# A two-layer graph kernel: the first layer in two parts, two list copies moved behind the first keys, later keys further ahead

## The chip, the cores and the metric

The kernel runs on one core of one Trainium2 chip. The metric is the device time of one execution in microseconds (us), lower is better. The kernel before has a median of 1617.65 us over three runs (1616.7 to 1618.55).

## The reference, cut to what matters

There are N = 6250 nodes with 64 features each, and E = 200000 edges given as two lists of integers, `src` and `dst`; `dst` is sorted. The first block is a two-layer SAGE network with a residual and a layer norm:

```
def sage_conv(x, src, dst, W_l, b_l, W_r, n_nodes):
    msg = x[src]
    agg = segment_sum(msg, dst, num_segments=n_nodes)
    cnt = segment_sum(ones, dst, num_segments=n_nodes)
    return agg / maximum(cnt, 1.0) @ W_l.T + b_l + x @ W_r.T
h   = relu(sage_conv(x, src, dst, W_l1, b_l1, W_r1, n))
x   = layernorm(x + sage_conv(h, src, dst, W_l2, b_l2, W_r2, n))
```

The second block has three message layers. Each sums `concat(x[dst], x[src], edge_attr) @ W.T + b` over the edges of every destination, with a batch norm between layers, a residual and a last layer norm. Every layer therefore sums over the same edges: five times the same sparse matrix, the count A[src, dst] of edges, is applied to node features.

## The kernel before, in words

**The matrix.** The kernel builds A once, as small 8-bit floats, in 13 tiles of 512 destinations each (`adj8`, in DRAM), and applies each tile to all nodes with matmuls (`aggregate`, line 664). Node features are held as three bf16 parts (`parts`), so that the sums stay exact enough.

**The build.** Edges are taken in slots of 128. One matmul per slot (line 1008) multiplies a one-hot of the low 7 bits of the source (`lo`) by a one-hot of a combined key of destination and high bits of the source (`rhs`), and adds into a PSUM pair of banks, `pair`; ScalarE copies a finished pair into the tile `a` (lines 1015 and 1020). VectorE makes the one-hots (`one_hots`, line 626) with a comparison of an iota with the keys, one instruction for 16 slots (`lo`) or for a run of slots (`rhs`). There are three buffers each of `lo` and `rhs`, and two of `pair`.

**The keys.** Slots go in 21 groups t of 128. For each group `fetch(t)` reads the edges (two gathers on GpSimd, DMA_INDIRECT of line 892), and `columns(t)` turns them into keys: four instructions on VectorE (lines 901 to 904), two TensorE transposes into `lin` (line 909) and one ScalarE copy into `k2` (line 911), which the one-hots read. Where each slot starts in the sorted list is searched at run time, in five steps of the list `SEARCH`: `near_samples` (line 826, then `pos` in line 834), `gather_behind` (GpSimd gathers, line 839), and `first_edges` (a comparison and sum per group, line 848, then `start_i` in line 860). `fetch(0)` reads the inputs `dst` and `src` themselves; later ones read padded copies of them in DRAM, `ends`, which two DMAs make at the start (line 798), one from the SP queue and one from the ACT queue. The features x come after the first keys (`load_x`, line 808, SP queue).

`on_slot` decides at which slot of which group these steps are called:

```
if c == (32 if t == 0 else 0):        # first_edges, fetch(t + 1), near_samples, gather_behind, gather_dst
...
if c == (96 if t == 0 else 64) and t + 1 < R:
    columns(t + 1)
```

**The first layer beside the build.** When step u of the build is written, the first SAGE layer of the tile finished before it follows in the source: `first_layer` aggregates (196 matmuls into `agg`), VectorE copies the counts (line 725), adds the three parts (line 689), divides (726, 727, 733); then four transposes (714), `lin` (736), a ScalarE relu (738), four matmuls (742) and a split into bf16 parts by ScalarE and TensorE in turn (636, 638). x itself is split the same way in `split_x` (line 882) between slots 64 and 192.

**Who sets the order.** The source order is not the order on the engines. A scheduler merges the program with a cost model of its own and may move an instruction past others of its engine; instructions wrapped in `pin` keep their order among themselves. Each engine then runs its instructions strictly in that fixed order and waits on semaphores. So the changed lines act through the order that results. The order of both programs on each engine is known before they run.

**After the build** (from about 485 us) come the last two first layers, the second SAGE layer with the edge attributes (to about 916 us), and the three message layers, which are almost nothing but matmuls.

Of the kernel before, what the change touches and what calls it, by code (L numbers as in the profile page):

```python
# [11 lines left out]
F32 = mybir.dt.float32  # L12
# [10 lines left out]
P = 128  # L23
# [451 lines left out]
def gnn_kernel(ctx: ExitStack, tc: tile.TileContext, x, src, dst, ea, W_l1, b_l1, W_r1, W_l2, b_l2, W_r2,  # L475
# [10 lines left out]
    nc = tc.nc  # L486
    pin = tc.keep_in_program_order
    N, D = x.shape
    E, EC = ea.shape
# [9 lines left out]
    def tw(j):  # L499
        return min(TW, NPAD - j * TW)  # L500
# [9 lines left out]
    R = -(-NS // P)  # L510
    subs = []
    for b in range(NB):
        n, c = slots_for(expected(N, E, b * P, (b + 1) * P)), 0
# [27 lines left out]

    dram = ctx.enter_context(tc.tile_pool(name="fdram", bufs=1, space=DRAM))
    ends = [dram.tile([E + PADE, 1], I32, name=f"ends{i}") for i in range(2)]
    adj8 = [dram.tile([P, NB * tw(j)], mybir.dt.uint8, name=f"adj8_{j}") for j in range(NT)]
    ok_t = None

    with ExitStack() as fast:
# [12 lines left out]
        parts = [const.tile([P, NB, 3 * D + 2], BF16, name="parts0"), const.tile([P, NB, 3 * D], BF16, name="parts1")]  # L560
# [157 lines left out]


        def first_layer(psa1, a, j):  # L720
            w, s = tw(j), slice(j * TW, j * TW + tw(j))
            nb, bs = w // P, j * TW // P
            ps, = aggregate(psa1, parts[0], [(a, j)], 3 * D + 1)
            c, ic = cnt[:, bs: bs + nb], inv[:, bs: bs + nb]
            nc.vector.tensor_copy(c, ps[:, :nb, 3 * D])
            nc.vector.tensor_single_scalar(ic, c, 1.0, ALU.max)
            nc.vector.reciprocal(ic, ic)
            nd = work.tile([P, 4, P], F32, name="nd")
            own_x = nc.scalar.copy(nd[:, :nb, D:], res[:, bs: bs + nb, :])
            if j == order[0][0]:  # L730
                pin(own_x)
            add_parts(nd[:, :nb, :D], ps, nb)
            nc.vector.tensor_mul(nd[:, :nb, :D], nd[:, :nb, :D], ic.unsqueeze(2).to_broadcast([P, nb, D]))
            mx = transposed_tile(nd, nb)
            ph = psm.tile([P, TW], F32, name="lin")
            nc.tensor.matmul(ph[:, :w], w1s, mx[:, :w], start=True, stop=True)
            h1 = work.tile([H1, TW], F32, name="h1")
            nc.scalar.activation(h1[:, :w], ph[:, :w], AF.Relu, bias=bl1)
            pz = psm.tile([P, 4, P], F32, name="tr")
            for i in range(nb):  # L740

                nc.tensor.matmul(pz[:, i, :], h1[:, i * P: (i + 1) * P], w2s, start=(i == 0), stop=True, skip_group_check=True)
            split_psum(parts[1][:, bs: bs + nb, :], pz[:, :nb, :D])
            nc.vector.tensor_add(res[:, bs: bs + nb, :], pz[:, :nb, D:], res[:, bs: bs + nb, :])


        with ExitStack() as bld:
# [15 lines left out]
            psa1 = slots.enter_context(tc.tile_pool(name="fpsa1", bufs=1, space=PSUM))  # L763
# [29 lines left out]
                pin(nc.scalar.dma_start(end[E:, :].rearrange("(p c) o -> p (c o)", p=64), pad[:64, i, :]))  # L793
            low = parts[1].rearrange("p b c -> p (b c)").bitcast(F32)
            early_weights = load_weights(low)
            for end, of, eng in ((ends[0], dst, nc.sync), (ends[1], src, nc.scalar)):

                pin(eng.dma_start(end[0: E, :].rearrange("(c p k) o -> p c (k o)", p=16, k=500),
                                  of.rearrange("(c p k) -> p c k", p=16, k=500)))
            nc.gpsimd.memset(parts[0][:, :, 3 * D: 3 * D + 1], 1.0)  # L800
            smf = pp.tile([EP, NSMP], F32, name="smf")
            nc.vector.tensor_copy(smf, smp)
# [1 line left out]
            def load_x():  # L804

                pin(nc.vector.memset(res[:, NB - 1, :], 0.0))
                pin(nc.vector.memset(res[:, :, 0:1], 0.0))
                pin(nc.sync.dma_start(res[:, : NB - 1, :], x[0: (NB - 1) * P, :].rearrange("(b p) d -> p b d", p=P)))
                pin(nc.sync.dma_start(res[:LASTB, NB - 1, :], x[(NB - 1) * P:, :]))
# [75 lines left out]
            cols, fetched, late_weights = {}, {}, []  # L885
# [10 lines left out]
            def columns(t):  # L896

                rows = fetched.pop(t)
                hi = ew.tile([P, P], I32, name="hi", bufs=1)
                key = ew.tile([P, 2, P], F32, name="key")  # L900
                pin(nc.vector.tensor_single_scalar(hi, rows[:, 1, :], 7, ALU.logical_shift_right))
                nc.vector.scalar_tensor_tensor(key[:, 0, :], rows[:, 0, :], float(NB), hi, ALU.mult, ALU.add)
                nc.vector.scalar_tensor_tensor(key[:, 1, :], hi, -float(P), rows[:, 1, :], ALU.mult, ALU.add)
                nc.vector.tensor_scalar(key[:, 0, :], key[:, 0, :], tab[:, 2, t: t + 1], 2000.0, ALU.subtract, ALU.min)  # L904
                if t == 0:
                    nc.vector.tensor_add(key[:, 0, :], key[:, 0, :], passed)
                kp = psm.tile([P, 2, P], F32, name="lin")
                for i in range(2):
                    nc.tensor.transpose(kp[:, i, :], key[:, i, :], ident)
                k2 = ew.tile([P, 2, P, 2], F16, name="k2")  # L910
                nc.scalar.copy(k2, kp.unsqueeze(3).to_broadcast([P, 2, P, 2]))  # L911
                cols[t] = k2, {}
                cols.pop(t - 2, None)

            def on_slot(slot):

                t, c = divmod(slot, P)
                if c == (32 if t == 0 else 0):
                    for g, (*_, t1) in enumerate(SEARCH):
                        if t == t1:  # L920
                            first_edges(g)
                            if g == len(SEARCH) - 1:
                                first_attributes()
                    if t + 1 < R:
                        fetch(t + 1)
                    for g, (_, _, t0, _) in enumerate(SEARCH):
                        if t == t0:
                            near_samples(g)
                            gather_behind(g)
                    gather_dst(t)  # L930
                if c == (96 if t == 0 else 64) and t + 1 < R:
                    columns(t + 1)
                    if t == 0:
                        for to, of in early_weights:
                            transposed(to, of)

                if t == SEARCH[-1][3] + 1 and c == 0:
                    free[0] = parts[1].rearrange("p b c -> p (b c)").bitcast(F32)
                    late_weights.extend(load_message_weights(spare))
                if t == SEARCH[-1][3] + 2 and c == 0:  # L940
                    for to, of in late_weights:
                        transposed(to, of)
                k = slot // HOT - 4
                if 0 <= k < 8 and c % HOT == 0:
                    n = -(-NB // 4)
                    split_x(k * n // 8, (k + 1) * n // 8)
# [5 lines left out]
            fetch(0)  # L952
            gather_behind(1)
            columns(0)
            load_x()
            pin(nc.sync.dma_start(thr[:, early:], t_ap[:, early:].to_broadcast([EP, P * (R + 1) - early])))
            pin(nc.sync.dma_start(etab, e_dram.ap() if hasattr(e_dram, "ap") else e_dram))

            def lo_hot(t, c):
                k2, made = cols[t]  # L960
                if c // HOT not in made:
                    lo = hot.tile([P, HOT, P], BF16, name="lo")
                    one_hots(lo, k2[:, 1, c // HOT * HOT: (c // HOT + 1) * HOT, :], iota)
                    made[c // HOT] = lo
                return made[c // HOT][:, c % HOT, :]

            built = {}

            def build(u):

# [5 lines left out]
                a = built[j]  # L976
# [21 lines left out]
                for e, (slot, wc, bank, col, first, last) in enumerate(todo):  # L998
                    t, c = divmod(slot, P)
                    wp = wc + wc % 2  # L1000
                    e0, g, i = of_run[e]
                    on_slot(slot)
                    if i == 0:
                        rhs = hot.tile([P, RUN], BF16, name="rhs")[:, : g * wp].rearrange("p (g n) -> p g n", n=wp)
                        one_hots(rhs, cols[t][0][:, 0, c: c + g, :], iota)
# [75 lines left out]
            for u, (j, _, _) in enumerate(order):  # L1081
                a = build(u)
                if u == 10:
                    relative_dst()
                if u == len(order) - 1:
                    break
                if prev is not None:
                    first_layer(psa1, *prev)
                    ready.append(prev[1])
                prev = (a, j) if a is not None else None  # L1090
            slots.close()
            psa = fast.enter_context(tc.tile_pool(name="fpsa", bufs=2, space=PSUM))
            psb = bld.enter_context(tc.tile_pool(name="psb", bufs=2, space=PSUM))
            for a, j in (prev, (a, j)):
                first_layer(psa, a, j)
                ready.append(j)


# [182 lines left out]
```

## Time and profile before

| | us |
|---|---|
| median of three runs | 1617.65 |
| the profiled execution, its own time | 1620.58 |
| span in that profile (first to last instruction) | 1618.8 |
| TensorE busy in the span | 1498.8 |
| VectorE busy | 886.1 |
| ScalarE busy | 574.3 |
| GpSimd busy | 226.9 |

The profiled execution lies 2.93 us, or 0.18%, above the median. "Busy" adds up the time in which an engine had an instruction running; a wait is written to the instruction that waited and to what ended the wait. The time of GpSimd's DMA_INDIRECT rows is the time in which it writes descriptors, not that of the transfer.

### The profile page before, as it was taken

To read this page: it belongs to the slowest core of one execution; us is meant where nothing else is said; L and a number is where in the kernel's file an instruction comes from. 1 tells how busy PE (TensorE), PEld (TensorE's weight loads), DVE (VectorE), ACT (ScalarE), POOL (GpSimd) and SP (SyncE) were. 2 spreads that over 40 slices of the span, in tenths; PEclk is the share of its full clock that TensorE was granted. 3 is DMA by queue.
4 is the path that set the end of the run, shared out by engine and by line. 5 is a ranking of instruction groups with operands and counts; after the bars stand their busy time and mean duration, and the time that the engine had idled before them with its cause. 6 is when DMAs were issued, how large, how long until landed. Compare 5 with 4: busy or idle time off the path is not lost.

```text
span 1618.8 us, 38661 instructions
## 1 busy us (share of the span) xinstructions
PE 1498.8 (93%) x17213; PEld 1384.0 (85%) x17213; DVE 886.1 (55%) x1462; ACT 574.3 (35%) x1080; POOL 226.9 (14%) x95
## 2 busy tenths in 40 slices
PE   3888799999998989999999999999999999999997
PEld 2676688888886888999899988889899999899997
DVE  6899998988969409987986511111431111442222
ACT  3737476777848404544554100000310000310000
POOL 2565732731610100000000000000000000000000
PEclk9897899999999999999999999999999999899998
DMA  5312232320321635435344354443245444264540
GB/s 134 122 30 95 46 100 88 158 93 14 157 84 81 240 133 223 182 130 206 133 145 154 126 239 160 167 171 120 124 187 212 162 163 156 101 240 175 193 163 10
DMA packets 45200, 227.32 MB, mean 140 GB/s; under 512 B 23621, under 2 KB 31650, under 8 KB 37343
## 3 DMA queue, kind: packets, MB, share of 16 engines
q1 hardware_dynamic: 37965, 139.40, 22.9%
q10 hardware_dynamic: 4306, 78.10, 12.3%
q0 software_dynamic: 2752, 7.26, 1.5%
q8 instruction: 136, 2.23, 0.5%
q14 instruction: 41, 0.34, 0.1%
HBM read 183.77 MB, written 42.57 MB: 140 GB/s over the span
## 4 chain that ended last, share of the span: by engine, by line
PE 64%; DVE 17%; issue 8%; ACT 6%; DMA 3%; POOL 2%; DVEq 0%; ACTq 0%; POOLq 0%
PE agg L664 48%; DVE lo L626 7%; PE pair L1008 7%; ACT a L1015 3%; DVE rhs L626 2%; PE u L1161 2%; DVE e L1066 2%; PE bank L1075 1%; POOL parts L839 1%; DMA e<-in_edge_attr_dram 1%; PE agg L671 1%; DVE e L1068 1%; DMA a<-adj 1%; DVE nd L689 1%; PE lin L1182 1%
## 5 line engine op out<-in xcount | busy, mean ns | idle before, releaser
L664 PE MATMUL agg<-parts,a 128*128 128x192 bf16 (+1 forms) x12005 | 1091.9, 246 | 6.3 <-DMA a<-adj 4.2
L664 PEld LDWEIGHTS <-a 128*128 128x128 fp8e3 x12005 | 1007.9, 98 | 25.7 <-issue 12.1
L1015 ACT ACTIVATE a<-pair 128x784 fp8e3<-128x784 f32 (+3 forms) x355 | 294.4, 900 | 107.2 <-PE pair L1008 85.8
L1008 PE MATMUL pair<-rhs,lo 128*128 128x147 bf16 (+5 forms) x2569 | 263.3, 239 | 45.0 <-ACT a L1015 15.3
L1008 PEld LDWEIGHTS <-lo 128*128 128x128 bf16 x2569 | 194.4, 101 | 98.8 <-issue 50.3
L626 DVE TENSOR_TENSOR rhs<-iota,k 128x1960 bf16<-128x1960 f16 (+15 forms) x240 | 239.2, 1018 | 18.3 <-ACT k L911 10.5
L626 DVE TENSOR_TENSOR lo<-iota,k 128x2048 bf16<-128x2048 f16 x161 | 195.3, 1217 | 1.9 <-ACT k L911 1.3
L689 DVE TENSOR_REDUCE z<-agg 128x256 f32<-128x768 f32 (+1 forms) x39 | 35.3, 910 | 282.6 <-PE agg L664 282.3
L892 POOL DMA_INDIRECT rows<-ends,start_i x40 | 142.6, 3564 | 177.6 <-DVE key L904 150.1
L626 DVE TENSOR_TENSOR lo<-iota,e_d 128x2048 bf16<-128x2048 f16 (+11 forms) x132 | 130.9, 1011 | 19.7 <-PE bank L1075 17.6
L1075 PE MATMUL bank<-lo,lhs 128*128 128x128 bf16 x1701 | 107.5, 219 | 18.0 <-ACT lhs L1069 12.6
L1075 PEld LDWEIGHTS <-lhs 128*128 128x128 bf16 x1701 | 98.3, 98 | 29.6 <-ACT lhs L1069 20.8
L689 DVE TENSOR_REDUCE nd<-agg 128x256 f32<-128x768 f32 (+1 forms) x26 | 23.5, 906 | 116.0 <-PE agg L664 116.0
L1177 POOL TENSOR_TENSOR nd<-res,inv 128x256 f32<-128x256 f32 (+1 forms) x13 | 7.6, 588 | 557.5 <-DVE inv L1152 346.6
L1169 DVE BATCH_NORM_STATS2 stats<-hr 64x6 f32<-64x512 f32 (+1 forms) x26 | 17.0, 653 | 101.7 <-ACT hr L1184 80.4
L716 ACT COPY mx<-tr 128x512 f32<-128x512 f32 (+1 forms) x26 | 14.7, 565 | 162.5 <-PE tr L714 162.5
L705 ACT ACTIVATE sp_r<-z 128x256 f32<-128x256 f32 (+1 forms) x26 | 10.5, 403 | 172.2 <-DVE z L704 172.0
L1198 ACT ACTIVATE hr<-tr 64x512 f32<-64x512 f32 (+1 forms) x13 | 7.3, 565 | 179.9 <-PE tr L1197 179.9
L839 POOL DMA_INDIRECT parts<-in_dst_dram,pos x22 | 60.8, 2763 | 40.8 <-DVE pos L834 31.7
L1065 ACT CAST lhs<-e 128x512 bf16<-128x512 f32 (+21 forms) x72 | 36.1, 503 | 64.0 <-PE bank L1075 40.5
L1066 DVE TENSOR_TENSOR e<-e,lhs 128x512 f32<-128x512 f32 (+21 forms) x72 | 39.4, 551 | 15.2 <-ACT lhs L1065 14.9
L1069 ACT CAST lhs<-e 128x512 bf16<-128x512 f32 (+21 forms) x72 | 36.4, 505 | 23.0 <-DVE e L1068 22.5
(145 smaller groups left out, 817.7 us busy)
## 6 DMA issues: line engine op xcount, KB each, us to landing
a<-adj SPq DMA_DIRECT2D x24, 3136.0 KB, 15.3
a<-adj ACTq DMA_DIRECT2D x24, 3136.0 KB, 11.1
adj<-a SPq DMA_DIRECT2D x12, 3136.0 KB, 9.6
e<-in_edge_attr_dram SPq DMA_DIRECT2D x25, 256.0 KB, 5.0
a<-adj SPq DMA_DIRECT2D x4, 784.0 KB, 4.1
out_dram<-z SPq DMA_DIRECT2D x12, 128.0 KB, 6.0
e<-in_edge_attr_dram SPq DMA_DIRECT2D x7, 152.0 KB, 3.6
adj<-a SPq DMA_DIRECT2D x1, 784.0 KB
```

What stands on the lines that cost most here:

```text
L626: nc.vector.tensor_tensor(to.rearrange("p g (h two) -> p g h two", two=2), iota[:, :n].rearrange("p (h two) -> p h two", two=2).unsqueeze( ...
L664: nc.tensor.matmul(sums[k][:, i, :n], views[k][:, b, i * P: (i + 1) * P], pt[:, b, :n], start=(b == sources[0] and terms is None and not ( ...
L689: nc.vector.tensor_reduce(to, ps[:, :nb, : 3 * D].rearrange("p b (r d) -> p b d r", r=3), AX.X, ALU.add)
L839: pin(nc.gpsimd.indirect_dma_start(out=blks[t % most], out_offset=None, in_=dst.rearrange("(e o) -> e o", o=1), in_offset=bass.IndirectOff ...
L892: pin(nc.gpsimd.indirect_dma_start(out=rows[:, i, :], out_offset=None, in_=end, in_offset=bass.IndirectOffsetOnAxis(ap=start_i[:, t: t + 1 ...
L1008: nc.tensor.matmul(pair[:, bank % 2, col: col + wc], lo_hot(t, c), rhs[:, i, :wc], start=first, stop=last)
L1015: nc.scalar.activation(av[:, :, o: o + 2 * nd].rearrange("p h (two d) -> p h two d", two=2), pair[:, :, : nd * NB].rearrange("p two (d h) ...
L1065: nc.scalar.copy(lhs[:, :g, 0:EC], r)
L1066: nc.vector.tensor_sub(r, r, lhs[:, :g, 0:EC])
L1069: nc.scalar.copy(lhs[:, :g, 2 * EC:3 * EC], r)
L1075: nc.tensor.matmul(ps[:, :P], lhs[:, q, :], oh[:, q % HOT, :], start=(c == 0 and q == 0), stop=(i == last_b[b] and q == g - 1))
L1161: nc.tensor.matmul(u[:, i, :], y[:, i * P: (i + 1) * P], maps[n - 1], start=True, stop=True)
```

## The change

It has four parts.

1. `first_layer` now returns after the aggregation, and the rest of it (counts, mean, transposes, both linear maps, the split) is a function that is called a quarter of the way into the next step of the build. The copy of the counts is pinned.
2. The two copies of `dst` and `src` into `ends` are no longer issued at the start. They are issued after `columns(0)`, both on the SP queue, behind a small DMA that writes one column of the first keys to DRAM (`seen`) and so makes the SP queue wait for those keys. `load_x` follows them on the same queue.
3. In group 0, the step with `first_edges`, `fetch(1)` and `near_samples` is called at slot 16 and not at slot 32.
4. From group 9 on, the keys of the next group are made at slot 32 and not at slot 64.

```diff
+    seen = dram.tile([P, 1], F32, name="seen")
...
         def first_layer(psa1, a, j):
+            ps, = aggregate(psa1, parts[0], [(a, j)], 3 * D + 1)
+            return lambda: first_layer_rest(ps, j)
+
+        def first_layer_rest(ps, j):
             w, s = tw(j), slice(j * TW, j * TW + tw(j))
             nb, bs = w // P, j * TW // P
-            ps, = aggregate(psa1, parts[0], [(a, j)], 3 * D + 1)
             c, ic = cnt[:, bs: bs + nb], inv[:, bs: bs + nb]
-            nc.vector.tensor_copy(c, ps[:, :nb, 3 * D])
+            pin(nc.vector.tensor_copy(c, ps[:, :nb, 3 * D]))
...
-            for end, of, eng in ((ends[0], dst, nc.sync), (ends[1], src, nc.scalar)):
-
-                pin(eng.dma_start(end[0: E, :].rearrange("(c p k) o -> p c (k o)", p=16, k=500),
-                                  of.rearrange("(c p k) -> p c k", p=16, k=500)))
+            def copy_ends():
+
+                pin(nc.sync.dma_start(seen, cols[0][2]))
+                for end, of in zip(ends, (dst, src)):
+                    pin(nc.sync.dma_start(end[0: E, :].rearrange("(c p k) o -> p c (k o)", p=16, k=500),
+                                          of.rearrange("(c p k) -> p c k", p=16, k=500)))
...
-                cols[t] = k2, {}
+                cols[t] = k2, {}, key[:, 0, 0:1]
...
-                if c == (32 if t == 0 else 0):
+                if c == (16 if t == 0 else 0):
...
-                if c == (96 if t == 0 else 64) and t + 1 < R:
+                if c == (96 if t == 0 else 64 if t < 9 else 32) and t + 1 < R:
...
             columns(0)
+            copy_ends()
             load_x()
...
                     on_slot(slot)
+                    if e == len(todo) // 4 and rest:
+                        rest.pop()()
...
                 if prev is not None:
-                    first_layer(psa1, *prev)
+                    rest.append(first_layer(psa1, *prev))
                     ready.append(prev[1])
                 prev = (a, j) if a is not None else None
+            for r in rest:
+                r()
...
             for a, j in (prev, (a, j)):
-                first_layer(psa, a, j)
+                first_layer(psa, a, j)()
                 ready.append(j)
```

More of the change, by code (lines that the diff above doesn't have):

```diff
@@ L959, in lo_hot @@
             def lo_hot(t, c):
-                k2, made = cols[t]
+                k2, made, _ = cols[t]
                 if c // HOT not in made:
@@ L967, in gnn_kernel @@
             built = {}
+            rest = []
             def build(u):
```

## The prediction, made before the changed kernel ran

> **What bounds the kernel now.** I read the windows first, because the change touches only the first 485 us and a mean over the kernel would hide it. Columns: stretch, its length, busy time (and count) of TensorE, weight load, VectorE, ScalarE, GpSimd, then the granted TensorE clock, DMA share and GB/s.
>
> ```profile
> 0.00:22.00 22.00, 2.40 (x22) 1.44 (x22) 6.15 (x35) 1.87 (x2) 8.67 (x19) 1.00 0.43 126
> 22.00:80.00 58.00, 45.10 (x414) 33.34 (x414) 50.27 (x79) 39.84 (x78) 24.80 (x15) 0.88 0.43 131
> 80.00:190.00 110.00, 88.61 (x1099) 74.77 (x1100) 108.04 (x172) 53.54 (x69) 69.83 (x22) 0.88 0.18 59
> 190.00:485.00 295.00, 283.16 (x3115) 252.15 (x3114) 260.52 (x318) 210.71 (x315) 107.44 (x25) 0.99 0.26 97
> ```
>
> To 22 us nothing is busy: a chain of small steps and DMAs leads to the first keys. From 22 to 190 us VectorE is the limit (158.3 of 168 us); TensorE idles 34 us there. From 190 us TensorE is (283 of 295). So a microsecond won at the start or on VectorE before 190 us should reach the end; one won on VectorE later should not. The waits of TensorE from 190 to 485 us confirm it: it waits for VectorE 1.6 us in all, in four rows.
>
> ```profile
> PE agg L664 <- DVE nd L689: 0.8, 2, 0.6
> PE pair L1008 <- DVE lo L626: 0.6, 2, 0.4
> PE tr L638 <- ACT parts L636: 0.2, 1, 0.2
> PE pair L1008 <- DVE rhs L626: 0.2, 1, 0.2
> ```
>
> Then the timeline of VectorE and GpSimd where VectorE does wait before 80 us (start, length, engine, what; in brackets the wait):
>
> ```profile
> 6.44 1.26 POOL L839 DMA_INDIRECT parts<-in_dst_dram,pos  x1 [3.66 <-DVE ext L826]
> 13.58 0.63 DVE L848 TENSOR_SCALAR_CACHE_REDUCE parts<-parts,tab 128x400 bf16<-128x400 int32 x1 [5.25 <-DMA parts<-in_dst_dram,pos]
> 16.54 0.94 POOL L892 DMA_INDIRECT rows<-in_src_dram,start_i  x1 [0.30 <-issue]
> 19.01 0.29 DVE L901 TENSOR_SCALAR hi<-rows 128x128 int32<-128x128 int32 x1 [3.59 <-DMA rows<-in_src_dram,start_i]
> ...
> 39.24 3.81 POOL L892 DMA_INDIRECT rows<-ends,start_i  x1 [16.76 <-DVE start_i L860]
> 45.83 0.28 DVE L901 TENSOR_SCALAR hi<-rows 128x128 int32<-128x128 int32 x1 [3.60 <-DMA rows<-ends,start_i]
> ...
> 66.65 6.58 POOL L839 DMA_INDIRECT parts<-in_dst_dram,pos  x1 [0.30 <-issue]
> 79.60 0.63 DVE L848 TENSOR_SCALAR_CACHE_REDUCE parts<-parts,tab 128x400 bf16<-128x400 int32 x1 [2.20 <-issue]
> ```
>
> Three waits count: 5.25 us for the first gather, 3.60 us for the edges of group 1, 2.20 us for the fifth gather of the third search step.
>
> **The change part by part.** The sum is against the profiled execution's own 1620.58 us (span 1618.8, so 1.8 outside it); that execution is 2.93 us above the median of 1617.65, and I carry the difference over to the median.
>
> *Copies behind the first keys.* The first gather's descriptors are ready at 6.44 + 1.26 = 7.70 us, and VectorE gets the data at 13.58: 5.9 us. The gather of 16.54 is ready at 17.48 and read at 19.01: 1.5 us, for 64 KB; the first gather moves 200 KB, so add some 0.7 us at the 200 to 300 GB/s that the DMA view shows: ready near 9.9 us. The DMA view of 8 to 11 us, then of 11 to 13.1 us, says why it was late (queue: packets, MB, share of the engines):
>
> ```profile
> q1 hardware_dynamic: 371, 0.70, 68.5%
> q10 hardware_dynamic: 122, 0.24, 26.1%
> ```
>
> ```profile
> q10 hardware_dynamic: 250, 0.49, 73.0%
> q0 software_dynamic: 64, 0.20, 26.4%
> ```
>
> q1 and q10 carry the two copies, q0 the gather, which moves nothing until q1's copy is done. [...] I take the trace: **3.6 us saved** (2.0 as the low end). The rest of the chain to the keys moves up with it. Of what is issued: the ACT queue loses one issue of 0.99 us, with ScalarE idle until 21 us: nothing. The SP queue gets `seen`, both copies and then x, behind a wait for the keys; behind them stand x, thresholds, `etab`. x is first used at 38.94 us (line 882), and the new order puts that use behind all slots of group 0, so later x (some 7 us of copies ahead of it) is covered. The copies themselves are needed by `fetch(1)`.
>
> *Step at slot 16.* In the new order of VectorE `start_i` for group 1 stands two `lo` and two `rhs` one-hots earlier (4.6 us by their 1.22 and 1.16 us rows), so GpSimd is asked at about 31 and not 39 us. But behind it now follow twelve one-hots without a break, and only then `hi`. At 39.24 GpSimd's row lasted 3.81 us, three one-hots long, and ended only after VectorE had stopped at 42.2 to wait for it; at 66.65 it lasted 6.58, until line 848 ran. [...] I take the trace: **0**, high end 3.6 saved.
>
> There is a cost besides. The keys of group 1 used to be made with four one-hots and four line-826 instructions still to do; now the first one-hot of group 1 stands directly behind them. What follows the keys (two transposes, ScalarE's copy) took 1.46 us at the first keys (20.36 to 21.82), uncovered: **1.5 us lost**, up to 2.5 where TensorE or ScalarE is behind.
>
> *Third search step.* Line 826 moves eight instructions back, so `pos` is ready near 61 us where it was 59.15 + 0.16, while its readers come some 3 us earlier. Between lies the 3136 KB store of the first finished tile, and gathers behind it wait for it: today's fifth did. I expect the wait of 2.2 us to become about 2.7, at the first of the six rather than the fifth: **0.5 us lost** (0 to 3).
>
> *Fourth search step* (near 115 us): the counts and sums of the first layer, 0.15 + 0.95 us of VectorE that gave GpSimd its turn at 113.5, now come behind the five line-848 instructions: one gather late, **0.6 us lost** (0 to 2).
>
> *Rest of the first layer.* The same instructions, about 15 to 30 slots later. Before 190 us VectorE is the limit, and its sum is unchanged. After 190 us the first-layer rows of TensorE's waits hold 0.8 + 0.2 us, so no more than 1.0 can go; the pinned copy could make VectorE wait for an aggregation (13.9 us today, hidden because TensorE is the limit). **0.5 saved**, between 1 saved and 2 lost. At the end of the build (485 us on) the order is the same in both programs.
>
> *Later keys.* VectorE waits 10.6 us for `k2` after 190 us (two rows, 9.3 + 1.3), but TensorE only 0.8 us for one-hots: **0.8 saved at most; I take it**, down to 0.5 lost.
>
> Sum: 3.6 - 1.5 - 0.5 - 0.6 + 0.5 + 0.8 = 2.3 us. Own time 1618.3, median **1615.3**. A measurement of this kernel tells about 0.2%, 3.2 us, from no change, so the likeliest case is just inside "same".
>
> **The rivals.**
>
> *GpSimd gets its turn.* If the gathers of group 1 slip in between one-hots, the 3.60 us go too, and the uncovered 1.5 grow to 2.1 because TensorE is no longer rested: 3 us more, 1612.3. For it: at 59.58 and 61.49 us two gathers took 1.61 and 1.21 us amid one-hots. Against: 39.24, the same spot, did not.
>
> *The split of x becomes the limit.* The 39 steps of splitting x lay over groups 0 and 1; now they follow group 1's first slots. TensorE then has about 17 us of it (line 882 9 to 10, line 638 7.4), 10 us of slots and 4 of small matmuls, 31 us in all against VectorE's 27, and possibly at half clock after the 5 us pause. Three buffers absorb 2 to 3 us. Price 1 to 5 us: 1616 to 1620, at 3 us 1618.3, no change.
>
> *Slower: the fourth gather of the second step.* It is issued at 21.54 + 0.95 us, just behind x:
>
> ```profile
> q1 hardware_dynamic: 1070, 1.10, 104.0%
> q0 software_dynamic: 35, 0.07, 3.6%
> ```
>
> In 22.5 to 27.6 us x fills the engines and the gather waits. With the change both copies and x form one stretch of the SP queue, from about 19 to 31 us. Today line 848 reads that gather at 34.76; in the new order at about 27.4. If the gather waits only for the first copy, it lands near 25 and costs nothing; behind both copies, near 27.5; if behind x also, near 33: 5.6 us, 1620.9. It decides at a landing after 27.4.
>
> **How the numbers follow.** Forecast 45%, GpSimd's turn 23%, split of x 16%, fourth gather 16%. The forecast's own range is 1612.5 to 1617.5, a third of it faster by over 3.2 us; GpSimd's turn nearly always; split of x half same, half slower; fourth gather slower four times in five. Faster: 0.15 + 0.22, and 0.04 for gains of the later first layer that no row shows, 0.41. Slower: 0.08 + 0.13, and 0.02 for the high ends of the unknown costs together, 0.23. Same: the rest, 0.36. Range 1609.5 to 1621: the low end is GpSimd's turn with all of the other high ends, the top the fourth gather.
>
> **What would show it.** Line 848's first wait falls from 5.25 to about 1.7 us and the first keys come near 16.8 us. The wait of `hi` for group 1 stays near 3.6, with GpSimd's first `ends` row some 12 us long, and the next `rhs` waits 1.5 for `k2`; the rival has a row under 4 us and no wait. The fourth line 848 waits 0, or over 3 if the slower rival is right. At 190 us TensorE should be ahead by 1 to 3 us and stay so to the end. The forecast is wrong if line 848's first wait stays above 4 us, or if TensorE's waits from 190 to 485 us change by more than 2 us.

## The result, and the profile after

The changed kernel is slower: 1623.69 us median of nine runs (1620.7 to 1627.23), beside 1616.74 us for the kernel before in the same set (1613.51 to 1619.12). The ratio is 1.0048, 95% interval 1.0035 to 1.0062. Measured a second time, beside other runs of the kernel before, it is 1.0025 (1.0015 to 1.0035), so the size of the loss is known only as some 5 to 7 us. The forecast was 1615.3 us, range 1609.5 to 1621.0.

The profiled execution took 1625.83 us, span 1624.0. In the changed program the line numbers of the first half grow by one and later ones by up to thirteen: line 848 is now 855, 892 is 899, 901 is 908, 911 is 918, 725 is 729, 1008 is 1019. The windows of the changed kernel, in the columns of before:

```profile
0.00:22.00 22.00, 4.05 (x29) 2.43 (x30) 9.74 (x38) 2.08 (x3) 9.16 (x19) 1.00 0.39 63
22.00:80.00 58.00, 35.99 (x320) 25.66 (x319) 43.01 (x67) 36.32 (x66) 27.65 (x11) 0.82 0.50 151
80.00:190.00 110.00, 93.58 (x1154) 82.35 (x1154) 107.01 (x172) 55.90 (x78) 56.69 (x24) 0.83 0.19 60
190.00:485.00 295.00, 278.44 (x3008) 246.27 (x3007) 262.07 (x324) 211.96 (x316) 120.50 (x24) 0.97 0.26 97
```

VectorE gains 3.6 us of work before 22 us and loses 7.3 in the next stretch. The granted TensorE clock (third column from the end) is 0.82, 0.83 and 0.97, where it was 0.88, 0.88 and 0.99. The timeline of the changed kernel's VectorE and GpSimd names the waits:

```profile
9.98 0.63 DVE L855 TENSOR_SCALAR_CACHE_REDUCE parts<-parts,tab 128x400 bf16<-128x400 int32 x1 [1.66 <-DMA parts<-in_dst_dram,pos]
15.42 0.28 DVE L908 TENSOR_SCALAR hi<-rows 128x128 int32<-128x128 int32 x1 [3.61 <-DMA rows<-in_src_dram,start_i]
17.94 0.94 POOL L846 DMA_INDIRECT parts<-in_dst_dram,pos  x1 [0.30 <-issue]
31.68 0.63 DVE L855 TENSOR_SCALAR_CACHE_REDUCE parts<-parts,tab 128x400 bf16<-128x400 int32 x1 [4.39 <-DMA parts<-in_dst_dram,pos]
35.70 12.86 POOL L899 DMA_INDIRECT rows<-ends,start_i  x1 [16.82 <-DVE start_i L867]
51.38 0.25 DVE L908 TENSOR_SCALAR hi<-rows 128x128 int32<-128x128 int32 x1 [3.63 <-DMA rows<-ends,start_i]
53.76 1.16 DVE L627 TENSOR_TENSOR rhs<-iota,k 128x1924 bf16<-128x1924 f16 x1 [1.40 <-ACT k L918]
77.39 0.63 DVE L855 TENSOR_SCALAR_CACHE_REDUCE parts<-parts,tab 128x400 bf16<-128x400 int32 x1 [3.93 <-DMA parts<-in_dst_dram,pos]
```

The first wait fell from 5.25 to 1.66 us, as forecast. The new one is the 4.39 us at 31.68: the fourth gather of the second search step, whose descriptors were written by 18.88, is there to be read 12.8 us later. In the DMA view from 18.5 to 26 us (queue: packets, MB, share) the reason is not full engines:

```profile
DMA packets 152, 0.36 MB, mean 47 GB/s; under 512 B 16, under 2 KB 113, under 8 KB 152
q1 hardware_dynamic: 97, 0.19, 40.0%
q0 software_dynamic: 55, 0.16, 29.5%
```

Both queues have work, and together they move 47 GB/s. From 26 to 31 us the same two queues make 302. Something slows the packets for some 8 us.

The second loss is seen where VectorE and TensorE change places as the limit. Aligned on the one-hots (start of the same `lo` in both traces) the changed kernel is 3.5 us behind near 204 us (the 65th `lo`) and 9.7 behind near 259 us (the 81st). The windows of that place, 3.4 us each:

```profile
197.50:200.90 3.40, 1.71 (x20) 1.19 (x18) 3.40 (x6) 2.63 (x4) 3.40 (x1) 1.00 0.12 15
200.90:204.30 3.40, 2.14 (x17) 1.96 (x17) 3.40 (x4) 1.65 (x3) 3.40 (x1) 0.50 0.12 13
204.30:207.70 3.40, 3.08 (x24) 2.46 (x21) 3.40 (x6) 3.12 (x5) 3.10 (x2) 0.50 0.15 20
207.70:211.10 3.40, 3.40 (x25) 3.14 (x24) 3.40 (x6) 1.52 (x2) 3.10 (x2) 0.50 0.27 48
```

TensorE is half idle, VectorE full; after a window with TensorE busy for 1.71 of 3.40 us its clock is 0.50 for three windows. The kernel before had 3 us of half clock between 190 and 250 us, this one has 14. Of what TensorE waits for from 190 to 485 us, VectorE's rows grew from 1.6 to 5.8 us, and all rows together from 9.7 to 16.0, more than the 2 us at which the prediction called itself wrong. VectorE's rows:

```profile
PE pair L1019 <- DVE rhs L627: 3.5, 4, 1.8
PE pair L1019 <- DVE lo L627: 1.6, 4, 0.6
PE agg L665 <- DVE nd L690: 0.7, 3, 0.3
```

Behind the build the lag is 11.9 us (at the 163rd `lo`, 545 us before), and 5.5 of it come back by the 164th (611 us). There the kernel before's own profile held a half-clock stretch of 6.8 us (clock 0.96 from 570 to 650 us, against 1.00 after). Between these two `lo` lie 65.6 us before and 60.2 after, and 59.5 to 60.4 with part 1, 3 or 4 alone, so I don't credit it to the change.

### The profile page after: what moved, and what is told of

It reads as the page before. It is cut to its first block, busy times and chain, and to the rows that moved or that the text cites. A ratio compares the mean times of both kernels' runs of the same rounds, so it can differ in the third digit from the quotient of the medians.

```text
span 1624.0 us, 38648 instructions
## 1 busy us (share of the span) xinstructions
PE 1502.6 (93%) x17213; PEld 1390.6 (86%) x17213; DVE 886.1 (55%) x1462; ACT 575.2 (35%) x1080; POOL 231.4 (14%) x95
## 4 chain that ended last, share of the span: by engine, by line
PE 53%; DVE 12%; ACT 3%; issue 3%; DMA 3%; DVEq 0%; ACTq 0%
PE agg L665 43%; DVE lo L627 4%; PE pair L1019 2%; PE u L1174 2%; DMA e<-in_edge_attr_dram 2%; PE bank L1086 1%; DVE e L1077 1%; PE agg L672 1%; DVE e L1079 1%; ACT a L1026 1%; DMA a<-adj 1%; PE lin L1195 1%; DVE nd L690 1%; DVE z L690 1%; PE lin L1196 1%
## 5 line engine op out<-in xcount | busy, mean ns | idle before, releaser
L1019 PE MATMUL pair<-rhs,lo 128*128 128x147 bf16 (+5 forms) x2569 | 268.6, 241 | 53.7 <-ACT a L1026 17.6
L1019 PEld LDWEIGHTS <-lo 128*128 128x128 bf16 x2569 | 199.0, 103 | 105.1 <-issue 51.8
L899 POOL DMA_INDIRECT rows<-ends,start_i x40 | 176.3, 4406 | 174.5 <-DVE key L911 141.9
L690 DVE TENSOR_REDUCE nd<-agg 128x256 f32<-128x768 f32 (+1 forms) x26 | 26.8, 1033 | 116.0 <-PE agg L665 116.0
L1076 ACT CAST lhs<-e 128x512 bf16<-128x512 f32 (+21 forms) x72 | 36.1, 502 | 62.3 <-PE bank L1086 39.7
L1078 ACT CAST lhs<-e 128x512 bf16<-128x512 f32 (+21 forms) x72 | 36.3, 505 | 23.3 <-DVE e L1077 21.7
L1080 ACT CAST lhs<-e 128x512 bf16<-128x512 f32 (+21 forms) x72 | 36.3, 505 | 23.0 <-DVE e L1079 22.5
```

The source lines that it names most:

```text
L690: nc.vector.tensor_reduce(to, ps[:, :nb, : 3 * D].rearrange("p b (r d) -> p b d r", r=3), AX.X, ALU.add)
L899: pin(nc.gpsimd.indirect_dma_start(out=rows[:, i, :], out_offset=None, in_=end, in_offset=bass.IndirectOffsetOnAxis(ap=start_i[:, t: t + 1 ...
L1019: nc.tensor.matmul(pair[:, bank % 2, col: col + wc], lo_hot(t, c), rhs[:, i, :wc], start=first, stop=last)
L1076: nc.scalar.copy(lhs[:, :g, 0:EC], r)
L1078: nc.scalar.copy(lhs[:, :g, EC:2 * EC], r)
L1080: nc.scalar.copy(lhs[:, :g, 2 * EC:3 * EC], r)
```

## The experiments

Each set of runs has its own runs of the kernel before, whose medians lay between 1614.75 and 1622.04 us; so ratios are compared within a set: from one set to another the same changed kernel moved from 1.0048 to 1.0025. Within a set differences of under 0.15% are not read. Three theories:

- A: the fourth gather, called four one-hots earlier by part 3, meets the copies of part 2.
- B: the pinned counts of part 1 come seven one-hots later, so `agg`, which has one buffer in PSUM, is freed later, and the next aggregation can't fill TensorE while VectorE is the limit.
- D, formed after the second set: it is not the copies that slow the gather but `seen`, 128 writes of 4 bytes into 512 bytes of DRAM.

The rivals: one part alone makes the whole loss; or there is only one loss, born early, and part 1 merely lies where it becomes visible.

### First set: each part alone

The kernel before with one of the parts of the diff shown above.

> The kernel before with part 1 alone (first layer in two parts, counts pinned). Theory A (the loss of 7 us is born in the second and third search steps, where gathers come late, and is then enlarged by TensorE's half clock): part 1 takes no part in it, 1616 to 1618, and the half clock before 500 us adds up to about 50 us as before. Theory B (the 5 to 6 us lost near 205 to 240 us come from the later rest of the first layer): 1621 to 1623, with a half-clock stretch near 200 us.

> The kernel before with part 2 alone (both copies behind the first keys). First keys 3.6 us earlier. The fourth gather of the second step is read after twelve one-hots, about 32 us, and lands near 30: no wait there. Theory A: what is left is the uncovered wait for k2 (1.4) and the late third search step (about 1.7 more than before); 1615.5 to 1618, same as before. Theory C (the copies alone, by their effect on the order and on the queue, make the whole loss): 1622 to 1625.

> The kernel before with part 3 alone (slot 16 for slot 32). The copies are out of the way by 13 us and x lands by 28 us, so the fourth gather should be there when it is read near 31 us. start_i four one-hots earlier, hi as before eighteen one-hots in: theory A says the wait of 3.6 us for the edges of group 1 shrinks or stays, 1613 to 1617. If the earlier step by itself is what hurts (GpSimd shut out longer): 1619 to 1622.

> The kernel before with part 4 alone (later keys at slot 32 from group 9 on). All theories: TensorE waits under 1 us for late keys there, so 1616 to 1617.5, no difference. A loss of over 2 us would say that the earlier keys push other VectorE work behind.

| part alone | ratio to before | interval |
|---|---|---|
| 1, first layer in two parts | 1.0026 | 1.0012 to 1.0040 |
| 2, copies behind the keys | 1.0002 | 0.9990 to 1.0015 |
| 3, slot 16 | 1.0003 | 0.9987 to 1.0020 |
| 4, later keys | 0.9980 | 0.9965 to 0.9996 |

Part 1 costs by itself (its median is 1626.53 us, beside 1620.65 and 1621.59 with part 2 or 3 alone), as theory B says. The windows from 200 to 210 us, the copy of the counts and the first matmuls of the next aggregation in the timeline, first with part 4 alone, whose program is there the same as before, then with part 1 alone:

```profile
200.00:210.00 10.00, 8.85 (x89) 7.19 (x89) 9.64 (x13) 7.34 (x14) 2.16 (x3) 1.00 0.20 35
199.21 0.15 DVE L726 COPY cnt<-agg 128x4 f32<-128x4 f32 x1
200.28 0.33 PE L665 MATMUL agg<-parts,a 128*128 128x193 bf16 x2 [0.58 <-DVE nd L690]
```

```profile
200.00:210.00 10.00, 6.53 (x60) 5.49 (x61) 10.00 (x15) 7.68 (x11) 9.70 (x2) 0.83 0.14 21
206.98 0.15 DVE L729 COPY cnt<-agg 128x4 f32<-128x4 f32 x1
209.00 1.26 PE L665 MATMUL agg<-parts,a 128*128 128x193 bf16 x13
```

The two kernels are together at the 65th `lo` (205.1 and 204.8). But with part 1 the counts come 7.8 us later, the next aggregation starts 8.7 us later, close behind the sum of the three parts in both, and TensorE does 60 matmuls in the window instead of 89. The 81st `lo` is at 258.6 instead of 252.3. With part 1 TensorE shows no wait for `agg` there: the fixed order already puts the aggregation behind the later slots, and meanwhile TensorE waits for one-hots and for ScalarE's copies of `pair`.

Part 2 alone has the slow copies too (149 packets from 18.5 to 26 us, 44 GB/s) and part 3 alone leaves them at the start; each alone is as fast as before. With slot 32 the fourth gather is read at 31.6 and waits 0.51 us. So the 4.39 us need both: part 2 slows the gather, part 3 brings its reader forward. (With part 1 undone, in the second set, parts 2, 3 and 4 show the wait at 4.27 us; the pair of parts 2 and 3 was not run by itself.) The four ratios add up to 1.0011; the changed kernel has 1.0025 to 1.0048.

Part 4 gains more than the 0.8 us of the forecast: 0.2% would be 3 us, the interval begins at 0.6. From the 105th `lo` (332 us) to the 163rd, its trace gains 2.3 us on that of part 3 alone (215.0 and 217.3 us).

This set also shows how far one profile reaches. With part 4 alone, the same program up to there, VectorE waits 3.05 us at 74.9 us for TensorE's split of x and is 6.4 us later at the 17th `lo` than in the profile of before that the prediction worked from. Beside this profile the changed kernel would not be behind at the 65th `lo` (203.8 and 205.1 us), and 7.0 us behind at the 81st.

### Second set: one loss taken out of the changed kernel

Part 1 undone (the diff above, backwards); counts first:

```diff
+            ps, = aggregate(psa1, parts[0], [(a, j)], 3 * D + 1)
...
+            nc.vector.tensor_copy(c, ps[:, :nb, 3 * D])
+            nd = work.tile([P, 4, P], F32, name="nd")
+            add_parts(nd[:, :nb, :D], ps, nb)
+            return lambda: first_layer_rest(nd, j)
```

and the copies behind the fourth gather, with part 1 and with part 1 undone:

```diff
-                pin(nc.sync.dma_start(seen, cols[0][2]))
+                pin(nc.sync.dma_start(seen, blks[(SEARCH[1][1] - 1) % most][:, 0:1].bitcast(F32)))
```

> The changed kernel with part 1 undone (first layer in one piece again). Theory B (the pinned counts come seven one-hots later, the only PSUM buffer of agg is freed later, so the next aggregation cannot fill TensorE while VectorE is the limit, near 200 us, and TensorE drops to half clock): the jump near 205 to 240 us goes, some 4 us less than the changed kernel, ratio to the kernel before 1.001 to 1.003; the step of -3.6 to about +4 us before 85 us stays. Rival (all of the loss follows from the late start, part 1 only falls where it is seen): ratio stays at 1.004 to 1.006 and the jump stays.

> The changed kernel with the cut of part 1 moved: counts and sum of the three parts (all that reads agg) directly behind the aggregation as before, and only the mean, the transposes and what follows a quarter into the next step. Theory B says that only the late release of agg costs: the jump near 205 to 240 us goes as in the run with part 1 undone, TensorE's half clock between 190 and 250 us falls from 14 us to under 7, ratio 1.001 to 1.003. Rival (the later transposes, linear maps and splits collide with slots): the jump stays, ratio 1.004 to 1.006.

> The changed kernel with seen reading the data of the fourth gather of the second search step instead of the first keys, so that both copies and x start only when that gather has landed. Theory A (the fourth gather stands behind the copies): its wait of 4.4 us on VectorE goes to 0, the first keys stay near 15.4 us, about 3 us less than the changed kernel: ratio 1.002 to 1.004 since part 1's loss stays. Rival 1 (x comes too late then, or the copies collide with the edges of group 1): a new wait of 2 to 5 us before 60 us, ratio 1.004 to 1.006. Rival 2 (the wait costs nothing since TensorE limits later): ratio unchanged at 1.005 though the wait is gone.

> Both remedies together: part 1 undone, and both copies and x behind the fourth gather. If theories A and B hold and add up, 7 us less than the changed kernel: ratio 0.999 to 1.0005. If the two losses are one (TensorE's half clock follows from the early lag, whatever the cause): the same as the better of the two single remedies.

| changed kernel with | ratio to before | interval |
|---|---|---|
| part 1 undone | 1.0026 | 1.0013 to 1.0039 |
| counts first | 1.0022 | 1.0012 to 1.0032 |
| copies behind the fourth gather | 1.0040 | 1.0027 to 1.0053 |
| the same, part 1 undone | 1.0029 | 1.0018 to 1.0041 |

The changed kernel was not run in this set, so these ratios by themselves don't show what each remedy is worth. In the traces B holds. With part 1 undone the counts come at 198.0 and the jump is gone; with the counts first they come at 198.8, the half clock between 190 and 250 us is 5 us, and by the 89th `lo` the kernel is as early as with part 1 undone (281.9 and 280.4, against 291.8); at the 81st it was still 6.1 us later than that (256.2 and 250.1). So it is the late release of `agg` that costs, not the later transposes. (The counts are also no longer pinned in this version; pin and place were not tried apart.) Its window from 200 to 210 us, counts first:

```profile
200.00:210.00 10.00, 9.77 (x120) 8.85 (x119) 10.00 (x12) 7.83 (x11) 8.26 (x2) 1.00 0.20 35
```

Part 1 costs further on, too. From the 105th `lo` to the 163rd the kernel before and the versions with part 2 or 3 alone take 217.2 to 217.6 us, part 1 alone 219.3 and part 4 alone 215.0. The versions that have part 4 take 217.8 to 218.4 us with part 1 as written, 215.3 to 215.8 without it and 213.7 to 214.7 with the counts first. So in the changed kernel part 1 takes back what part 4 gains.

The gather's remedy missed, and with part 1 undone it is no better (1.0029) than part 1 undone alone (1.0026). The wait of 4.39 us is gone, but the edges of group 1, read from the copies, are later:

```profile
49.53 0.23 DVE L908 TENSOR_SCALAR hi<-rows 128x128 int32<-128x128 int32 x1 [6.19 <-DMA rows<-ends,start_i]
```

The copies, now alone on the engines, still crawled: from 22.7 to 30.7 us they moved 0.34 MB, 42 GB/s. No gather was in flight. What all slow stretches have in common is what goes ahead of them, `seen`.

### Third set: the small writes

```diff
-    seen = dram.tile([P, 1], F32, name="seen")
+    seen = dram.tile([1, P], F32, name="seen")
...
-                cols[t] = k2, {}, key[:, 0, 0:1]
+                cols[t] = k2, {}, key[0:1, 0, :]
```

This writes the 512 bytes from one partition; the wait for the first keys stays. The second run has part 1 undone as well. The third is the kernel before with `pin(nc.sync.dma_start(seen, cols[0][2]))` ahead of x in `load_x`. The fourth takes `key[: P // 2, 0, 0:1]`, 64 writes.

> The changed kernel with seen written as one row of 512 bytes from one partition instead of 128 writes of 4 bytes; everything else, the wait for the first keys too, as it was. Theory D (the 128 small writes to one 512 bytes of DRAM clog the memory for about 8 us, so that both the copies and the fourth gather trickle at some 20 KB per us from 18 to 26 us): the copies run at over 200 KB per us from the start, end near 24 instead of 30.5 us, x ends near 31, the fourth gather lands before 27 us and VectorE's wait of 4.4 us is gone; about 3 us less than the changed kernel, ratio 1.003. Rival (queue order: the gather waits for the copies' packets whatever precedes them): the trickle from 18 to 26 us stays, and the wait of 4.4 us with it.

> Part 1 undone and seen in one row: parts 2, 3 and 4 with the two losses taken out. If both remedies add up, ratio 0.998 to 1.0005. What is left against the kernel before: first keys 3.6 earlier, the uncovered k2 1.4, the third search step. If the ratio stays near 1.0025, as with part 1 undone alone, the gather's wait did not reach the end.

> The kernel before with nothing but the 128 writes of 4 bytes (one column of the first keys to DRAM) put ahead of x on the SP queue; copies at the start as before. Theory D: x trickles for 8 us and ends near 36 instead of 28 us, and the fourth gather of the second step, which is issued behind it, is late or slow too. Rival (the trickle belongs to the copies, which read the list that the gathers read): x moves at some 210 KB per us as before and ends near 29 us.

> The changed kernel with seen from 64 partitions instead of 128: 64 writes of 4 bytes. Theory D by its dose: the trickle lasts about 4 us instead of 8, from 18 to 22 us, the fourth gather lands near 23 to 25 and VectorE's wait falls from 4.4 us to 0 to 1. Rival (queue order): no change, 4.4 us.

One row: 0.9976 (0.9966 to 0.9985); with part 1 undone 0.9970 (0.9956 to 0.9984). In the DMA view from 18.5 to 26 us, seen in one row, the crawl is gone:

```profile
DMA packets 1195, 2.21 MB, mean 294 GB/s; under 512 B 64, under 2 KB 1111, under 8 KB 1195
q1 hardware_dynamic: 1079, 1.85, 90.9%
q0 software_dynamic: 116, 0.35, 14.5%
```

The fourth line 855 runs at 27.16 us without a wait. The kernel before with the small writes shows the same from the other side. Its DMA from 22.5 to 28 us, and that of the kernel before without them:

```profile
DMA packets 393, 0.48 MB, mean 87 GB/s; under 512 B 16, under 2 KB 362, under 8 KB 393
```

```profile
DMA packets 1187, 1.26 MB, mean 228 GB/s; under 512 B 16, under 2 KB 1167, under 8 KB 1187
```

Here it is x, going into SBUF, that crawls behind the writes, and the fourth gather makes line 848 (850 there) wait 1.13 us where it waited for nothing. (One execution, 1623.85 us: no ratio.) The rivals that blamed the copies or the order of the queues are out. The theory's dose is not borne out: with half the writes (one execution as well) 168 packets passed from 18.5 to 25 us, and the fourth gather still made VectorE wait:

```profile
30.61 0.63 DVE L855 TENSOR_SCALAR_CACHE_REDUCE parts<-parts,tab 128x400 bf16<-128x400 int32 x1 [3.20 <-DMA parts<-in_dst_dram,pos]
```

I had expected 0 to 1. Half the writes did not halve the slow stretch.

### Fourth and fifth set: what each is worth, and the best version

The changed kernel and its one-row version again, side by side; one row with parts 1 and 3 undone (slot 32); one row with the counts first. Then the last once more, beside one row with part 1 undone.

> The changed kernel once more, beside the next three, because the ratio of the run with seen in one row (0.9976) was taken on other runs of the kernel before than the 1.0048 of the changed kernel. If the 128 small writes cost what the two ratios say, this one is 0.4 to 0.7% above the one-row version here too (ratio 1.002 to 1.005). If the ratio differs with the runs it is taken beside: near 0.999, and the small writes are worth only the 4.4 us of the trace, 0.25%.

> The changed kernel with seen in one row once more. Trace-based: 4.4 us of VectorE's wait plus what TensorE's half clock makes of it, 6 to 8 us less than the changed kernel beside it; ratio to the kernel before 0.997 to 0.999.

> Parts 2 and 4 alone, with seen in one row: slot 32 as before, first layer in one piece. start_i for group 1 comes four one-hots later and hi stays 23 one-hots in, so GpSimd has less time, but its row should again last until VectorE stops. If part 3 is worth nothing (the step at slot 16 only lengthens GpSimd's row): the same as parts 2, 3 and 4 with one row, ratio 0.996 to 0.998. If the earlier step is worth something here: 2 us more, 0.998 to 0.9995.

> The changed kernel with both remedies that keep its four parts: seen in one row, and counts and sum read from agg directly behind the aggregation, the rest a quarter into the next step. Theory B and D add up: 1 to 4 us less than seen in one row alone, ratio 0.996 to 0.998, TensorE's half clock from 190 to 250 us under 6 us. Rival (part 1 costs nothing any more once VectorE is on time): the same as seen in one row alone.

> Seen in one row and counts first, once more: its ratio of 0.9944 stood on six executions (1610 to 1617 us) while its trace ends only 1.6 us before that of seen in one row alone. If the ratio is right: 0.994 to 0.996 again. If it was the small number: 0.997 to 0.998, and no better than one row with part 1 undone.

> Seen in one row with part 1 undone, once more and beside the version that keeps part 1 with the counts first: 0.997 before. If part 1's later transposes are worth something of their own once agg is freed in time, this is 2 us or more slower than the version beside it; if part 1 brings nothing, the two are the same within 2 us.

| | median, us | ratio to before | interval |
|---|---|---|---|
| changed kernel | 1625.21 | 1.0025 | 1.0015 to 1.0035 |
| one row | 1619.19 | 0.9986 | 0.9974 to 0.9997 |
| one row, parts 1 and 3 undone | 1618.22 | 0.9979 | 0.9966 to 0.9992 |
| one row, counts first (6 executions) | 1613.41 | 0.9944 | 0.9925 to 0.9962 |
| fifth set: one row, counts first | 1614.94 | 0.9958 | 0.9943 to 0.9973 |
| fifth set: one row, part 1 undone | 1616.49 | 0.9970 | 0.9957 to 0.9983 |

One 512-byte write for 128 small ones is worth 6.0 us here by the medians, 0.39% by the ratios. In the first pair of traces (the changed kernel and one row of the third set) 4.5 us of it stand at 38 us (the 5th `lo`), 6.5 at the 89th (near 290 us) and 7.9 at the end of the span. What is added lies from 218 us on, just behind the place where TensorE sits at half clock for 7 us instead of 14 between 190 and 250 us; no run separates the clock's share from the rest. Window 200 to 210 us, one row and then one row with the counts first:

```profile
200.00:210.00 10.00, 9.32 (x91) 8.24 (x90) 10.00 (x15) 7.78 (x10) 9.39 (x3) 0.76 0.18 27
```

```profile
200.00:210.00 10.00, 9.58 (x118) 8.72 (x116) 10.00 (x14) 9.12 (x11) 4.43 (x2) 1.00 0.18 27
```

The fastest version keeps all four parts with one row and the counts first: 0.9958, some 6 us under the kernel before. Whether part 1 is then better than no part 1 (1614.94 against 1616.49 us) isn't shown: the difference lies inside the intervals. Part 3 is worth nothing that can be told: 0.9970 with it and 0.9979 without, in different sets.

## Why the prediction was wrong, by its own steps

Two steps failed: `seen` was put at nothing where, with part 3 in place, it costs 6.0 us, and the rest of the first layer was put at 0.5 us saved where it costs 2 to 6.

- *Copies behind the first keys, 3.6 saved*: right for the first wait. It is 1.66 us, and the first keys start at 15.42 where they started at 19.01. So what I took from the trace of before held: from 8 to 11 us q1 and q10 had 68.5 and 26.1% of the DMA engines there, and the gather's queue moved nothing. For the low end of 2.0 no run shows a ground. **The same step failed in its last part**: it counted `seen` only as a wait, and what stands behind it as covered. `seen` is a DMA of 128 writes of 4 bytes, and behind it the copies took from 18 to some 31 us (q1 moved 1.50 MB in that time) where the step gave them some 7.
- *Step at slot 16, 0*: right in size. GpSimd's row lasts 12.86 us, to 48.56, VectorE stops at 47.75, and the wait of `hi` is 3.63, as the rows of 3.81 and 6.58 us in the trace of before let expect.
- *Uncovered `k2`, 1.5 lost*: right, 1.40. The 2.1 of the rival of GpSimd's turn was my estimate, and its reason points the wrong way: in the trace of before the two transposes took 0.66 us at 20.50, where TensorE had rested for 12.75 us, and 0.44 at 47.90, where it had for 1.68.
- *Third search step, 0.5 lost*: mis-sized. The wait is 3.93 us and not 2.7, so 1.7 lost, inside its 0 to 3, and at the first of the six as foreseen. That the store makes it wait was not tested.
- *Fourth search step, 0.6 lost*: no wait, 0. The fifth step's two waits of before (1.42 and 0.53 us) went away, unforeseen, but three new waits of VectorE for TensorE and ScalarE between 86 and 190 us (0.72, 1.59 and 0.68) took their place.
- *The slower rival, the fourth gather at 16%*: it came true, 4.39 us in one profile and 5.37 in another against its price of 5.6. Its point of decision, a landing after 27.4 us, was right; its cause was not, so that its price was met was luck. With `seen` written as one row the rival's wait is gone: the queues were not the trouble. The bound "if the gather waits only for the first copy, near 25" was sound for the copies alone.
- *Rest of the first layer, 0.5 saved, between 1 saved and 2 lost*: **this step failed**. I bounded it by TensorE's waits after 190 us, taken as rows that could only shrink, and looked for the cost of the pin on VectorE. (Of those waits I read four rows as VectorE's; the 1.6 us are three, the fourth is a wait for ScalarE.) What the later counts hold is `agg`: until they and the sum have been read, the next tile's 196 matmuls cannot start, and those fill TensorE exactly while VectorE is the limit. The ratio of part 1 alone puts 2 to 6 us on it; where only part 1 was taken out of a version with the other parts, the medians moved by 2.1 and 2.3 us (third and second set), which is at the edge of the noise.
- *Later keys, 0.8 saved*: mis-sized; the part alone has 0.9980, some 3 us, though its interval begins at 0.6.
- *Left out near 200 us*: TensorE's clock, which the prediction has only in the rival on the split of x. The half clock that this rival holds possible came: in the changed kernel TensorE had no work from 49.53 to 52.42 us, and its clock was 0.50 from 50.8 us for 10.2 us. Up to 650 us the half-clock stretches in the traces of the two kernels last 3.4, 6.8 or 10.2 us (to within 0.2), and one of the changed kernel 13.6. Near 200 us it was 10.2, behind a window of 3.40 us with 1.71 us of work; what brings the clock down was not shown. A few us lost on VectorE near 200 us may have become more on TensorE; how much is open.
- *The sum*: with the measured terms its sign changes. 3.6 saved, less 1.4 for `k2`, 1.7 for the third search step, 4.4 for the gather and 2 to 6 for `agg`, with 0.8 for the later keys, is 5 to 9 slower (an estimate); 5 to 7 were measured. With `seen` in one row and nothing else mended the ratio is 0.9976 in one set and 0.9986 in another; the forecast's 2.3 us would be 0.9986. That it comes so near is luck: part 1's loss is still in it, and so are gains that the forecast did not have.

## What to carry to other kernels

A DMA that serves only as a signal is still a DMA: `seen`, one column of 128 partitions, was 128 writes of 4 bytes, and 6.0 us here. Write such a signal as one row, and look at what moves behind it. Before an instruction that reads a single-buffered PSUM tile is moved back, ask which matmuls wait for that buffer and whether they fill an engine that is about to become the limit (the 196 into `agg` here, 2 to 6 us by the ratio of part 1 alone). Two edits that each cost nothing that can be told (1.0002 and 1.0003 here) can make a wait together (4.39 us) when one delays a transfer and the other brings its reader forward, so try the parts alone and in pairs.

## What the runs showed of the hardware

- Behind 128 writes of 4 bytes to DRAM from 128 partitions (in the changed kernel q1 shows 144 packets under 512 bytes, 0.00 MB, from 17 to 18.5 us) the transfers of the core's queues crawled: 42 to 87 GB/s over the windows of 5.5 to 8 us shown above, where the like transfers made 228 to 294 without these writes. It was so for copies in DRAM, for x going into SBUF and for a gather of GpSimd's queue. Behind 64 writes they made 62 GB/s, behind one write of 512 bytes 294. Whether it is the size of the writes, that they share the same 512 bytes, or that they are spread over the partitions was not tried.
- In the changed kernel TensorE's clock fell to 0.50 after a 3.40 us window in which it was busy for 1.71 us (197.50 to 200.90), and stayed there for 10.2 us. The 1.71 us alone don't decide it: in the trace of before, TensorE was busy for 1.71 us of the window from 77.17 to 80.58 us, and the clock stayed at 1.00 in the next.
- GpSimd, writing descriptors while VectorE made one-hots, took 12.86 us (35.70 to 48.56) for a row that takes 0.94 elsewhere in the same trace, and ended only after VectorE had stopped, at 47.75, to wait for it. With part 2 or part 3 alone such a row took 8.45 and 8.23 us.
